# A planned four-layer graph network on one core: pair sums by transfers and VectorE norms in the last batch, setup work with its own priorities

## The chip, the cores and the metric

The kernel runs on one core of one Trainium2 chip. The metric is the device time of one execution in microseconds (us). A core has five engines that run their own instruction streams and wait for each other by semaphores: TensorE (PE, matmuls), VectorE (DVE), ScalarE (ACT), GpSimd (POOL) and SyncE (SP, which only issues transfers). All data are float32.

## The reference

Sixteen graphs (a batch each) of 1024 nodes with 256 features share one adjacency matrix of 1024 x 1024. Three graph attention layers with 4, 1 and 1 heads are followed by one transformer block with 8 heads; each layer gets the normalized, rectified features and is added to its input. Cut to what matters:

```python
def gat(h, adj, W, a, heads, slope, act):
    q = (h @ W).reshape(B, N, heads, D)
    e = (q . a_src)[:, :, None, :] + (q . a_dst)[:, None, :, :]
    e = where(adj > 0, leaky_relu(e, slope), -inf)
    return act(einsum('bijh,bjhd->bihd', softmax(e, axis=2), q))

def block(x, adj):
    q, k, v = split(x @ w_qkv)               # 8 heads of 32
    s = where(adj > 0, q @ k.T / sqrt(32), -1e9)
    x = layernorm(x + softmax(s) @ v, ln1_g, ln1_b)
    f = relu(x @ w1 + b1) @ w2 + b2
    return layernorm(x + f, ln2_g, ln2_b)

for layer in (gat0, gat1, gat2, block):      # elu, relu, elu, -
    x = x + layer(max(layernorm(x), 0))
```

## The kernel before

One function, `direct`, records the work of all sixteen batches, operation by operation, with the engine, an estimated duration, what is written and what is read (`pe`, `act`, `dve`, `pool` and `dma`, all by `Record.add`). `Record.schedule` (L193) then makes one order out of it: a list scheduling in which each engine takes, of the work that its model calls ready, the piece with the smallest key. The instructions are emitted in that order, so all queues stand as the planner left them. A key (`priority`, L140) is the batch number plus a value read off a line of knots by the position in the stream, minus a `LEAD` for the engine. The streams are `gat0`, `gat1`, `gat2` (the graph layers), `beside` (the first layer of batch 1, put beside batch 0), `steps` and `values` (the attention), `feed` (the second half of the block) and `last` (that half in the last batch). `PASS` is the delay that the model assumes between engines, `SLACK` an addition to a transfer's landing, `BIAS` the weight of a turn of PE between its tilings (whole array, or four columns of 32, called `col4`). The streams of the setup have fixed knots: weights of layer 0 and the adjacency (`setup`), weights of the others (`setup_later`), `signs`.

Two batches overlap: while one is in its graph layers, which multiply 128x128 weights by whole rows (L825 projections, L951 sums over neighbours in layers 1 and 2, L1038 and L1048 in layer 0), the other is in its attention. A graph layer hands to the next through `hn` (normalized rows, ACT, L533), PE transposes (L562), `hT` (their copies, ACT, L819), and the projection (L825), from which ACT makes the node terms `e` (L836) and `rt` (L897).

The attention of a batch has 32 steps: 2 head groups g of 4 heads, 2 halves hf of the query nodes, 8 blocks jt of 128 key nodes. A step makes four score products (L1417), their exponentials on ACT (L1441) into two tiles of 128x1024 from the ring `r_pa`, two multiplications by the mask on DVE (L1450), and one quad of 32-column products with the values (L1274). The denominators are quads of the same kind against a tile of ones. `run_of` (L1282) says how many steps one such quad serves: 8 in most batches, for which DVE adds tiles (L1301, L1309) and GpSimd issues accumulating transfers (L1318) into `sums`; 1 in the last batch, which adds nothing and issues a ones quad in each step.

After the attention `feed` normalizes (`turn`), makes the two products (L1517) and adds. `back` then turns each pair of row tiles back: transposes into a PSUM bank, copies with a row sum on ACT (L1609), squares on ACT (L479), the inverse root (L491 on DVE, L499 on POOL), and for each row tile a product with the gain (L1628) and one that adds the row of `xr` (L1641), which a transfer brought from DRAM (L1577) and L1583 adds a constant to. A last transfer stores it (L1650).

Behind the planned order stand a few instructions that make a flag from range checks: a matmul into the first shared PSUM bank (L1754), a sum and a comparison on DVE (L1756, L1757). All engines load the flag (L2309) and branch around a general version, which does not run here.

Of the kernel before, what the change touches and what calls it, by code (L numbers as in the profile page):

```python
# [16 lines left out]
AF = mybir.ActivationFunctionType  # L17
# [99 lines left out]
PASS = {"pe": 0.184, "act": 0.255, "dve": 0.2, "pool": 0.13, "dma": 0.0}  # L117
# [30 lines left out]
class Record:  # L148
# [165 lines left out]
SLACK = 0.962  # L314
KNOTS = {
# [3 lines left out]
    "beside": (-5.886, -0.218, 3.926, -4.339, 3.82),  # L319
    "values": (-2.1, -3.167, -2.515, -3.878, -1.376, 0.819, 4.772, 4.031, -0.727),  # L320
    "steps": (-0.731, 1.092, 1.111, 1.525, 1.942, 1.949, 3.509, 2.697, 0.422),
    "feed": (2.466, 7.301, 1.215, 1.509, 2.436, 1.431, -2.979, 1.844, 1.385),
    "last": (5.718, 3.017, 3.751, 2.762, 4.403, 4.069, 2.002, 6.755, 6.465),
}
BIAS = 3.565
LEAD = {"act": 3.258, "dve": -0.77}
# [33 lines left out]
def direct(ctx, tc, flag, x, adj, gat_w, gat_a, w_qkv, ln1_g, ln1_b, ln2_g, ln2_b, w1, b1, w2, b2, out):  # L360
# [328 lines left out]
    def signs():  # L689

        rec.stream(0, (0.9, 1.6), False)
        for it in range(NT):
            again = r_yT.new()
            a_i = again.t.rearrange("p a n -> p (a n)").bitcast(I32)
            dma(
                1.8,
                1.7,
                lambda: nc.sync.dma_start(a_i, adj[it * P : (it + 1) * P, :]),
                [again],
                [],  # L700
            )
# [436 lines left out]
    def attention(b, xt, b_mv, b_rstd):  # L1138
# [131 lines left out]
        pas, accs, sums = {}, {}, {}  # L1270
# [11 lines left out]
        def run_of(g, hf):  # L1282

            return 1 if b == NB - 1 else NT
# [4 lines left out]
        for n in range(len(steps) + LAG):  # L1289
            m = n - LAG  # L1290
            if m >= 0:
# [4 lines left out]
                if jt % run == 1:  # L1296
# [106 lines left out]
            if n < len(steps):  # L1403
# [5 lines left out]
                pts = [r_pa.new() for _ in range(2)]  # L1409
# [50 lines left out]
        watch(b_rec, b_rec.t, 1)  # L1460
        return hn

    def feed(b, x3, hn):
# [105 lines left out]
        def back(hf):  # L1569
            yT = yTs[hf]  # L1570
            for it in (hf * TH, hf * TH + 2):
# [34 lines left out]
                for k in range(2):  # L1606
                    act(
                        act_us(C) + 100e-3,
                        lambda: nc.scalar.activation(  # L1609
                            z_t[:, k, :], pz()[:, k, :], AF.Copy, accum_out=mvz.t[:, k, 0:1]  # L1610
                        ),
                        [z(k), mvz(k)],
                        [g],
                    )
                refs = [mvz(0), mvz(1)]
                spread_of(
                    [z_t[:, k, :] for k in range(2)],
                    [z(k) for k in range(2)],
                    mvz.t[:, :, 0],
                    mvz.t[:, :, 1],  # L1620
                    refs,
                )
                inverse_of_squares(mvz.t[:, :, 0], mvz.t[:, :, 1], rstdz.t, refs, rstdz, False)
                for k in range(2):
# [12 lines left out]
                        [mvz(k)],  # L1637
# [26 lines left out]
    def begin(b):  # L1664
# [3 lines left out]
        for hf in range(2):  # L1668
# [7 lines left out]
                b - 1.0,  # L1676
# [47 lines left out]
    graph(0, states[0], 0, first=True)  # L1724
# [626 lines left out]
```

## Time and profile before

| what | us |
|---|---|
| three runs | 3969.0, 3971.94, 3972.6 |
| median | 3971.94 |
| the profiled execution | 3968.2 |
| its span in the profile | 3966.4 |
| PE, from its first matmul to its last | 12.59 to 3955.56 |
| a period of the middle (two overlapping batches) | 241 |

The span runs from the first to the last event of the profile, and 1.8 us of the execution's time lie outside it. The mean granted clock of PE is 0.997 of full speed. Times in the views count from the start of the span. PEld is the weight load of PE, which runs beside its matmuls. The end of a matmul is modelled in the profile, so a wait can hide in a record that looks long. The groups that the change touches, in the list by costliest group and in the list of transfers (columns: line, engine, operation, tiles and shapes, count, then busy us, mean ns, then idle ahead of it and what ended it; for transfers the size of one and the us to its landing):

```profile
L1441 ACT ACTIVATE pa<-sc 128x512 f32<-128x512 f32 x2048 | 1099.7, 602 | 375.4 <-PE sc L1417 263.7
L1450 DVE TENSOR_TENSOR pa<-pa,mask 128x1024 f32<-128x1024 f32 x1024 | 1225.3, 1215 | 84.2 <-ACT pa L1441 83.0
L1318 POOL DMA_DIRECT2D sums<-pa x360 | 317.4, 882 | 1124.1 <-DVE pa L1450 324.5
L1274 PE MATMUL bank<-pa,va 128*32 128x512 f32 x4096 | 533.4, 599 | 1.0 <-DVE pa L1450 1.0
...
sums<-pa POOLq DMA_DIRECT2D x360, 512.0 KB, 5.0
```

### The profile page before, as it was taken

The numbers are of one execution on the slowest core, as the hardware profiler recorded it, in microseconds if no ns is written. First come the engines' busy times: TensorE is split into PE (matmuls) and PEld (weight loads), VectorE is DVE, ScalarE is ACT, GpSimd is POOL, SyncE is SP. The second block draws the span as 40 slices with busy tenths as digits, with TensorE's granted clock in tenths as the row PEclk, the third lists the DMA queues.
The fourth block names the chain that finished last, engine by engine and source line by source line (L and its number), as shares of the span: only waits on it lengthen the run. The fifth ranks groups of instructions, "written<-read, shape, count | busy, mean of one in ns | idle before, by whom it ended". The sixth has DMA issues, their size and how long they took to land. (4 is left out here: it accounts for less than half of the span.)

```text
span 3966.4 us, 64316 instructions
## 1 busy us (share of the span) xinstructions
PE 3915.6 (99%) x22946; PEld 2325.5 (59%) x22946; DVE 3616.0 (91%) x6134; ACT 2659.1 (67%) x6643; POOL 819.1 (21%) x751
## 2 busy tenths in 40 slices
PE   8999999999999999999999999999999999999998
PEld 4566566564665646566565665646656465665644
DVE  7769998999989999999999989999899999999976
ACT  5367577675766757577675776757667575775676
POOL 1002122221212212122121222212122131221210
PEclk9999999999999999999999999999999999999999
DMA  3156575555745556465465755557455564654652
GB/s 132 46 144 140 129 168 120 134 128 129 172 115 135 131 126 157 118 164 124 118 146 131 165 120 133 130 129 171 117 131 132 129 157 118 158 123 111 148 133 69
DMA packets 245946, 523.55 MB, mean 132 GB/s; under 512 B 26736, under 2 KB 61808, under 8 KB 245616
## 3 DMA queue, kind: packets, MB, share of 16 engines
q1 hardware_dynamic: 193776, 330.58, 29.5%
q0 software_dynamic: 51840, 188.77, 24.7%
q8 instruction: 183, 3.00, 0.3%
q14 instruction: 147, 1.20, 0.1%
HBM read 229.45 MB, written 101.06 MB: 83 GB/s over the span
## 5 line engine op out<-in xcount | busy, mean ns | idle before, releaser
L1441 ACT ACTIVATE pa<-sc 128x512 f32<-128x512 f32 x2048 | 1099.7, 602 | 375.4 <-PE sc L1417 263.7
L1450 DVE TENSOR_TENSOR pa<-pa,mask 128x1024 f32<-128x1024 f32 x1024 | 1225.3, 1215 | 84.2 <-ACT pa L1441 83.0
L924 DVE SCALAR_TENSOR_TENSOR pt<-row,e,mask 128x512 f32<-128x512 f32 x1472 | 1011.5, 742 | 43.4 <-DMA row<-rd 33.0
L951 PE MATMUL bank<-qb,pt 128*128 128x257 f32 x4096 | 952.2, 381 | 3.8 <-ACT rt L897 3.2
L951 PEld LDWEIGHTS bank<-qb,pt 128*128 128x128 f32 x4096 | 770.1, 189 | 168.6 <-ACT pa L1441 12.6
L1417 PE MATMUL sc<-qs,ks 128*128 128x512 f32 x2048 | 743.6, 467 | 3.1 <-ACT pa L1441 2.8
L1318 POOL DMA_DIRECT2D sums<-pa x360 | 317.4, 882 | 1124.1 <-DVE pa L1450 324.5
L1274 PE MATMUL bank<-pa,va 128*32 128x512 f32 x4096 | 533.4, 599 | 1.0 <-DVE pa L1450 1.0
L1417 PEld LDWEIGHTS sc<-qs,ks 128*128 128x128 f32 x2048 | 368.6, 189 | 189.2 <-issue 73.0
L1038 PE MATMUL bank<-pt,qb 128*32 128x512 f32 x3840 | 462.4, 597 | 3.4 <-DVE rec L1094 2.9
L1309 DVE TENSOR_TENSOR sums<-sums,pa 128x1024 f32<-128x1024 f32 x360 | 433.9, 1215 | 9.8 <-DMA sums<-pa 9.2
L825 PE MATMUL bank<-w_aug,hT 128*128 128x259 f32 (+1 forms) x1504 | 376.2, 394 | 5.1 <-DVE w_aug L641 2.7
L825 PEld LDWEIGHTS bank<-w_aug,hT 128*128 128x128 f32 x1504 | 277.5, 191 | 124.3 <-ACT hT L819 19.1
L499 POOL TENSOR_TENSOR rstd<-rstd,neg_half 128x4 f32<-128x4 f32 x94 | 152.0, 1617 | 794.6 <-DVE rec L971 472.6
L1038 PEld LDWEIGHTS bank<-pt,qb 128*32 128x32 f32 x3840 | 114.7, 110 | 269.0 <-issue 204.3
L1274 PEld LDWEIGHTS bank<-pa,va 128*32 128x32 f32 x4096 | 110.5, 109 | 254.1 <-issue 215.9
L979 ACT ACTIVATE ex<-bank,rec 128x256 f32<-128x256 f32 x256 | 121.0, 478 | 203.8 <-DVE rec L971 203.0
L1048 PE MATMUL bank<-pt,e 128*32 128x512 f32 x1920 | 252.2, 592 | 0.0
L1188 PE MATMUL sc<-hTa,wqkv_sb 128*128 128x512 f32 x512 | 243.8, 599 | 0.7 <-ACT hTa L1173 0.3
L533 ACT ACTIVATE hn<-xh,mv,rstd 128x256 f32<-128x256 f32 x376 | 199.8, 597 | 12.2 <-DVE mv L523 10.5
L479 ACT ACTIVATE waste<-xh,mv 128x256 f32<-128x256 f32 x376 | 191.6, 510 | 8.2
L514 POOL TENSOR_TENSOR rstd<-rstd,neg_half 128x4 f32<-128x4 f32 x66 | 86.7, 1313 | 496.1 <-DVE rstd L511 488.2
(153 smaller groups left out, 4565.5 us busy)
## 6 DMA issues: line engine op xcount, KB each, us to landing
sums<-pa POOLq DMA_DIRECT2D x360, 512.0 KB, 5.0
ks<-hl SPq DMA_DIRECT2D x256, 256.0 KB, 4.4
qs<-hl SPq DMA_DIRECT2D x256, 256.0 KB, 4.8
row<-rd SPq DMA_DIRECT2D x184, 256.0 KB, 3.3
hl<-hi SPq DMA_DIRECT2D x128, 256.0 KB, 3.3
hl<-lo SPq DMA_DIRECT2D x128, 256.0 KB, 3.6
xh<-in_x_dram SPq DMA_DIRECT2D x32, 512.0 KB, 3.9
x<-xh SPq DMA_DIRECT2D x32, 512.0 KB, 2.7
```

The source lines that it names most:

```text
L825: nc.tensor.matmul(g.t[:, : C + 3 * H], hT.t[:, ct, k * P : (k + 1) * P], w_aug[l][:, ct, :], start=ct == 0, stop=ct == CT - 1,)
L924: lambda: nc.vector.scalar_tensor_tensor(pt.t, row.t, e3[:, 2, jt // TH, h, jt % TH : jt % TH + 1], mask[:, jt, hf * HALF : (hf + 1) * HAL ...
L951: nc.tensor.matmul(g.t[:, : D + 1], pts[jt].t[:, k * P : (k + 1) * P], qb[:, jt, 0, :], start=jt == 0, stop=jt == NT - 1,)
L1038: nc.tensor.matmul(g.t[u * D + d : u * D + d + D3, :], qb[:, j, h + u, d : d + D3], pts[u][j - jt].t, start=j == 0, stop=j == NT - 1,)
L1048: nc.tensor.matmul(gd.t[c : c + D3, :], one(jt + k, h + u).to_broadcast([P, D3]), pts[u][k].t, start=jt == 0, stop=jt == NT - 2,)
L1188: nc.tensor.matmul(sc.t, wqkv_sb[:, ct, c0 : c0 + P], hT.t[:, ct, hf * HALF : (hf + 1) * HALF], start=ct == 0, stop=ct == CT - 1,)
L1274: nc.tensor.matmul(ac.t[r * D3 : (r + 1) * D3, :], columns(r), of_head(r), start=first, stop=last,)
L1309: lambda: nc.vector.tensor_add(ss.t, ss.t, pt.t),
L1318: lambda: nc.gpsimd.dma_start(ss.t, pt.t, accum_op=ALU.add),
L1417: nc.tensor.matmul(scs[r - r0].t, ks.t[:, r, jt * P : (jt + 1) * P].bitcast(F32R), q.t[:, r, :].bitcast(F32R), start=True, stop=True,)
L1441: lambda: nc.scalar.activation(pt.t[:, v, :], sc.t, AF.Exp, scale=1.0 / math.sqrt(D3)),
L1450: lambda: nc.vector.tensor_mul(pt.t, pt.t, mask[:, jt : jt + 1, i0 : i0 + HALF].to_broadcast([P, 2, HALF]),),
```

## The change

There are four parts. The planner's constants and nearly all knots have other values, and the setup's streams have knots of their own: `prepare` (weights of layer 0), `flags` (the adjacency), `later`, `signs`, and `first` for the first layer of batch 0. The transfers that bring x for batch 0 have the key -9.0 and not -1.0. In the last batch `run_of` is 2 for the first head group: the tiles of an odd step are added to those of the even step by two accumulating transfers that GpSimd issues, 512 KB each, and one ones quad serves both; the even steps' tiles come from six tiles lent by rings that are no longer used by then. In the second head group a ones quad still serves one step. For the last two row tiles of the last batch (`whole`) DVE takes mean and variance from PSUM with bn_stats and bn_aggr, and the product with the gain reads PSUM and subtracts the mean; the two ACT copies and the two squares of that pair are gone.

```diff
--- before.py
+++ after.py
@@ -114,7 +114,7 @@
 
 
 WEIGHT = {"pe": 1.0, "dve": 0.3}
-PASS = {"pe": 0.184, "act": 0.255, "dve": 0.2, "pool": 0.13, "dma": 0.0}
+PASS = {"pe": 0.187, "act": 0.284, "dve": 0.216, "pool": 0.13, "dma": 0.0}
 
 
 class Port(float):
@@ -311,19 +311,24 @@
 
 
 BEHIND, HELD = 2.0, 1.35
-SLACK = 0.962
+SLACK = 0.878
 KNOTS = {
-    "gat0": (-10.592, -9.852, -9.404, -9.422, -4.685, -5.744, -2.501, -5.476, -8.387),
-    "gat1": (-1.314, -0.409, 0.269, 0.767, 0.801, 0.716, 1.107, 1.18, 1.068),
-    "gat2": (0.968, -0.933, -0.332, -0.095, 0.667, 0.376, 1.511, 2.244, 1.831),
-    "beside": (-5.886, -0.218, 3.926, -4.339, 3.82),
-    "values": (-2.1, -3.167, -2.515, -3.878, -1.376, 0.819, 4.772, 4.031, -0.727),
-    "steps": (-0.731, 1.092, 1.111, 1.525, 1.942, 1.949, 3.509, 2.697, 0.422),
-    "feed": (2.466, 7.301, 1.215, 1.509, 2.436, 1.431, -2.979, 1.844, 1.385),
-    "last": (5.718, 3.017, 3.751, 2.762, 4.403, 4.069, 2.002, 6.755, 6.465),
+    "prepare": (-8.171, -25.204, -1.219),
+    "flags": (-1.972, 28.969, 31.434),
+    "later": (-3.058, -13.974, -19.276),
+    "signs": (9.615, 1.252, 2.905),
+    "first": (-33.677, -26.463, -11.613, -10.505, -4.473, -51.659, -18.668, -16.537, -6.288),
+    "gat0": (-11.671, -11.56, -7.573, -11.755, -6.35, -7.559, -3.8, -7.279, -7.121),
+    "gat1": (-1.318, -0.26, 0.293, 0.732, 0.82, 0.753, 1.148, 1.366, 1.233),
+    "gat2": (0.538, -0.372, 0.011, -0.014, 0.518, 0.041, 1.546, 1.925, 1.743),
+    "beside": (-5.462, -0.695, 4.93, -2.997, 3.186),
+    "values": (-2.004, -2.881, -2.02, -3.934, -1.847, 0.835, 4.775, 3.429, -0.703),
+    "steps": (-0.94, 1.05, 1.057, 1.547, 1.962, 2.299, 2.791, 2.536, 1.391),
+    "feed": (2.215, 6.339, 2.027, 1.413, 2.389, 1.61, -3.1, 1.598, 2.903),
+    "last": (7.027, 1.257, 3.242, 4.245, 5.763, 6.015, 2.958, 7.404, 7.821),
 }
-BIAS = 3.565
-LEAD = {"act": 3.258, "dve": -0.77}
+BIAS = 3.466
+LEAD = {"act": 3.86, "dve": -1.129}
 
 SWITCH = {
     ("full", "col4"): 0.137,
@@ -688,7 +693,7 @@
 
     def signs():
 
-        rec.stream(0, (0.9, 1.6), False)
+        rec.stream(0, KNOTS["signs"], False)
         for it in range(NT):
             again = r_yT.new()
             a_i = again.t.rearrange("p a n -> p (a n)").bitcast(I32)
@@ -711,15 +716,15 @@
 
 
     def setup():
-        rec.stream(-3.0, (0.0, 1.0), False)
+        rec.stream(0, KNOTS["prepare"], False)
         prepare(0)
-        rec.stream(-0.9, (0.0, 0.1), False)
+        rec.stream(0, KNOTS["flags"], False)
         nat = r_ks.new()
         for it in range(NT):
             neighbours(it, nat)
 
     def setup_later():
-        rec.stream(-0.5, (0.0, 0.3), False)
+        rec.stream(0, KNOTS["later"], False)
         prepare(1)
         prepare(2)
         dma(
@@ -1267,7 +1272,14 @@
         b_rec = r_reca.new()
         rc = b_rec.t.rearrange("p (a b t h) -> p a b t h", a=CT, b=2, t=TH)
         steps = [(g, hf, jt) for g in range(CT) for hf in range(2) for jt in range(NT)]
-        pas, accs, sums = {}, {}, {}
+        pas, accs, sums, outs = {}, {}, {}, {}
+        r_even = r_pa
+        if b == NB - 1:
+            owners = [r_qb.new(), r_hT.new(), r_hn.new()] + [r_sums.new() for _ in range(2)]
+            t_qb, t_hT, t_hn, *more = (o.t for o in owners)
+            tiles = [t_qb[:, k * N : (k + 1) * N].rearrange("p (a n) -> p a n", a=2) for k in range(2)]
+            tiles += [t_hT, t_hn.rearrange("p t c -> p (t c)").rearrange("p (a n) -> p a n", a=2)] + more
+            r_even = Lent(tiles, owners)
 
         def quad(ac, of_head, columns, first, last):
             for r in range(HG):
@@ -1281,7 +1293,7 @@
 
         def run_of(g, hf):
 
-            return 1 if b == NB - 1 else NT
+            return (1 if g == 1 else 2) if b == NB - 1 else NT
 
         rec.stream(b, KNOTS["steps"])
         GROUP = 2
@@ -1293,7 +1305,19 @@
                 if jt == 0:
                     accs[g, hf] = [r_bank.new(), r_bank.new()]
                 run = run_of(g, hf)
-                if jt % run == 1:
+                if run == 2 and jt % 2:
+                    sums[g, hf] = pas[m - 1]
+                    for ss, pt in zip(pas[m - 1], pas[m]):
+                        dma(
+                            2.4,
+                            2.0,
+                            lambda: nc.gpsimd.dma_start(ss.t, pt.t, accum_op=ALU.add),
+                            [ss],
+                            [pt],
+                            us=1.135,
+                            engine="pool",
+                        )
+                elif jt % run == 1:
                     sums[g, hf] = [r_sums.new() for _ in range(2)]
                     for ss, p0, p1 in zip(sums[g, hf], pas[m - 1], pas[m]):
                         dve(
@@ -1406,7 +1430,7 @@
                     f(*at)
                 pas[n] = []
                 i0 = hf * HALF
-                pts = [r_pa.new() for _ in range(2)]
+                pts = [(r_pa if jt % 2 else r_even).new() for _ in range(2)]
                 pas[n] = pts
                 for r0 in range(0, HG, GROUP):
                     scs = [r_sc.new() for _ in range(GROUP)]
@@ -1458,6 +1482,8 @@
                                 mask_of(hf),
                             )
         watch(b_rec, b_rec.t, 1)
+        if b == NB - 1:
+            r_even.give_back()
         return hn
 
     def feed(b, x3, hn):
@@ -1603,38 +1629,47 @@
 
                 q = it % TH // 2 if PARTS == 2 else 0
                 pe(0.109 * 2 * CT, turn_back, [g], [yT((co, q)) for co in range(CT)])
-                for k in range(2):
-                    act(
...
-                inverse_of_squares(mvz.t[:, :, 0], mvz.t[:, :, 1], rstdz.t, refs, rstdz, False)
+                whole = PARTS == 2 and it == TH + 2
+                if whole:
+                    refs = [mvz(0), mvz(1)]
+                    for k in range(2):
+                        st = r_st["f"].new()
+                        dve(0.315, lambda: nc.vector.bn_stats(st.t, pz()[:, k, :]), [st], [g])
+                        dve(0.08, lambda: nc.vector.bn_aggr(mvz.t[:, k, :], st.t), [mvz(k)], [st])
+                    inverse(mvz.t[:, :, 0], mvz.t[:, :, 1], rstdz.t, refs, rstdz, False)
+                else:
+                    for k in range(2):
+                        act(
...
+                    inverse_of_squares(mvz.t[:, :, 0], mvz.t[:, :, 1], rstdz.t, refs, rstdz, False)
                 for k in range(2):
                     u, xs = z_t[:, k, :], xr.t[:, k, :]
                     dve(
                         stt_us(C),
                         lambda: nc.vector.scalar_tensor_tensor(
                             u,
-                            u,
+                            pz()[:, k, :] if whole else u,
                             mvz.t[:, k, 0:1],
                             rows["g2"][:, 0, :],
-                            op0=ALU.add,
+                            op0=ALU.subtract if whole else ALU.add,
                             op1=ALU.mult,
                         ),
                         [z(k)],
-                        [mvz(k)],
+                        [mvz(k)] + ([g] if whole else []),
                     )
                     dve(
                         stt_us(C),
@@ -1673,7 +1708,7 @@
                 lambda: nc.sync.dma_start(xt.half(hf), x_b[:, s, :]),
                 [xt(it) for it in range(hf * TH, (hf + 1) * TH)],
                 AFTER_ROWS[1 if b == 1 else 3] * (b in (1, 2)),
-                b - 1.0,
+                b - 1.0 if b else -9.0,
             )
         for hf in range(2):
             its = range(hf * TH, (hf + 1) * TH)
@@ -1721,7 +1756,7 @@
 
     setup()
     states = [begin(0)]
-    graph(0, states[0], 0, first=True)
+    graph(0, states[0], 0, knots=KNOTS["first"], first=True)
     setup_later()
     states.append(begin(1))
     borrowed = lent()
```

More of the change, by code (lines that the diff above doesn't have):

```diff
@@ L1605, in back @@
                 pe(0.109 * 2 * CT, turn_back, [g], [yT((co, q)) for co in range(CT)])
-                for k in range(2):
-                    act(
[L1608 to L1613, printed above, removed]
-                    )
[L1615 to L1622, printed above, removed]
-                inverse_of_squares(mvz.t[:, :, 0], mvz.t[:, :, 1], rstdz.t, refs, rstdz, False)
+                whole = PARTS == 2 and it == TH + 2
[9 more added lines that the diff above has]
+                        act(
+                            act_us(C) + 100e-3,
+                            lambda: nc.scalar.activation(
+                                z_t[:, k, :], pz()[:, k, :], AF.Copy, accum_out=mvz.t[:, k, 0:1]
+                            ),
+                            [z(k), mvz(k)],
+                            [g],
+                        )
+                    refs = [mvz(0), mvz(1)]
+                    spread_of(
+                        [z_t[:, k, :] for k in range(2)],
+                        [z(k) for k in range(2)],
+                        mvz.t[:, :, 0],
+                        mvz.t[:, :, 1],
+                        refs,
+                    )
+                    inverse_of_squares(mvz.t[:, :, 0], mvz.t[:, :, 1], rstdz.t, refs, rstdz, False)
                 for k in range(2):
```

## The prediction

> **What bounds the kernel now.** I read the busy times first, then the busy time by windows, then the waits of PE, then timelines of the places that the change touches. The busy times:
>
> ```profile
> PE 3915.6 (99%) x22946; PEld 2325.5 (59%) x22946; DVE 3616.0 (91%) x6134; ACT 2659.1 (67%) x6643; POOL 819.1 (21%) x751
> ```
>
> PE sets the time. Work taken from DVE, ACT or POOL is worth something only where PE waits for it. Where that is shows in the windows (columns: stretch, its length, then busy us and instructions of PE, PEld, DVE, ACT, POOL; then clock and DMA):
>
> ```profile
> 0.00:12.50 12.50, 0.00 (x0) 0.00 (x0) 7.81 (x38) 2.11 (x3) 1.78 (x8) 1.00 0.81 284
> 12.50:120.00 107.50, 97.89 (x743) 48.39 (x744) 88.88 (x184) 56.23 (x157) 10.60 (x12) 0.98 0.29 94
> 120.00:225.00 105.00, 101.16 (x577) 68.15 (x578) 76.61 (x168) 44.14 (x117) 5.73 (x10) 0.95 0.17 56
> 225.00:300.00 75.00, 71.01 (x306) 43.76 (x308) 48.52 (x70) 49.98 (x118) 8.08 (x11) 0.98 0.66 166
> ...
> 1140.00:1381.00 241.00, 240.72 (x1415) 143.81 (x1415) 226.12 (x381) 165.56 (x417) 54.83 (x48) 1.00 0.57 136
> ...
> 3750.00:3956.00 206.00, 200.06 (x1136) 103.51 (x1134) 154.02 (x250) 142.96 (x328) 21.32 (x21) 1.00 0.38 96
> 3956.00:3966.40 10.40, 0.00 (x0) 0.00 (x0) 4.69 (x12) 2.58 (x11) 2.16 (x2) 0.56 0.27 86
> ```
>
> A middle period of 241 us (13 alike) has PE idle for 0.28 us. The ends have idle: 12.5 ahead of the first matmul, 9.6 up to 120, 3.8 up to 225, 4.0 up to 300, 5.9 in the last 206, and 10.4 behind the last matmul. The waits of PE name the single causes (sum, times, longest):
>
> ```profile
> PE bank L562 <- DVE rstd L511: 12.6, 1, 12.6
> PE bank L951 <- ACT rt L897: 3.2, 13, 0.2
> PE bank L1038 <- DVE rec L1094: 2.9, 1, 2.9
> ...
> PE bank L825 <- DVE w_aug L641: 2.7, 1, 2.7
> PE bank L562 <- ACT hn L533: 1.8, 1, 1.8
> ```
>
> The sum is made against the profiled execution: 3968.2 us, of which the span is 3966.4; the median of the runs is 3971.94, 3.7 above it, and I add that at the end.
>
> **Start.** The key of the first loads moves x ahead of W and a on SP: two issues, at 0.76 and 1.26, so x is issued and lands 1.0 us sooner, and W and a as much later. DVE now does the row statistics ahead of the weight preparation, which stood ahead of them from 4.98 to 7.67. In the built order two groups of adjacency transposes on PE, not four, and two mask copies on ACT, not three, stand ahead of the first hT. The first exponentials of the node terms are now at:
>
> ```profile
> 20.44 2.02 ACT L681 CAST mask<-bank 128x512 uint8<-128x512 f32 x4
> 22.33 0.21 ACT L836 ACTIVATE e<-bank 128x12 f32<-128x12 f32 x1
> ```
>
> With the same durations in the new order: statistics start at 6.7 instead of 7.67; from the first to hn's shift (7.67 to 11.48) it was 3.81, less one statistic of 0.4, so hn starts at 10.2 instead of 11.67; its four take 2.07; eight transposes 1.04 and two copies 1.07 end at 14.4; the second hn group takes 2.07 and four mask copies 2.02, with 0.2 between, so the first e stands at 18.7: 3.6 us sooner. The first weighted adjacency (DVE L924, at 31.20) follows by the same step at 27.6. From there to 93 DVE is the slower engine (88.88 busy of 107.5), so the lead is carried. The preparation of layer 1's weights, for which PE waits 2.7 us at 119.86, now has 6.1 us less DVE work ahead of it by the sum of the two orders' durations (87.5 against 93.6), PE has 5.0 less ahead of its projection (84.6 against 89.6). I take −4.7 at that point: −3.6 from the head and 1.1 of the wait. Bounds: −1.0 (the x issue alone) and −6.1 (all of DVE's lead).
>
> Then batch 1's first-layer sums stand between batch 0's layers 1 and 2 in the new order, where PE waits 0.60 for e at 193.76 and 1.84 for hn at 195.87: −2.5 for both, bounds 0 and −4.0 (a further 1.5 of the slow L825 behind them). The stretch 225–300, where PE waits on exponentials, keeps nearly its order: 0, bounds ±4.0, its idle.
>
> **Middle.** All knots change, but the built PE order has 13 periods with the same work, 95% of it in the same places, DVE 87%, ACT 82%. The weak place is the handover from layer 1 to 2, where ACT makes hT between two groups of hn:
>
> ```profile
> 1323.53 1.29 PE L1417 MATMUL sc<-qs,ks 128*128 128x512 f32 x4
> 1324.75 2.06 PE L1274 MATMUL bank<-pa,va 128*32 128x512 f32 x8
> 1326.73 4.12 PE L825 MATMUL bank<-w_aug,hT 128*128 128x259 f32 x16
> ...
> 1324.17 0.56 ACT L819 COPY hT<-bank 128x512 f32<-128x512 f32 x1
> 1324.63 2.08 ACT L533 ACTIVATE hn<-xh,mv,rstd 128x256 f32<-128x256 f32 x4
> 1326.61 0.56 ACT L819 COPY hT<-bank 128x512 f32<-128x512 f32 x1
> ```
>
> The quad pair of 8 at 1324.75 shows 2.06, and elsewhere 1.07 (at 1317.97): 0.99 is a hidden wait for the copy at 1326.61. The new order places that copy behind the same hn group, and one exponential more (0.60) ahead of the first copy, while it takes the first half's transposes earlier. I take 0. Bounds: 13 × −0.99 = −12.9, and 13 × 0.60 = +7.8.
>
> **Fewer denominators.** For the first head group of the last batch a ones quad (4 columns × 2 records) is issued every second step: 8 quads fewer of 16. A chain of waits gives the price: "PE bank L1274" x16 takes 1.85, x24 2.71, so 0.86 for 8: 8 × 0.86 = −6.9. They ran in a stretch where PE is 97% busy, so this counts in full. Two more visits to the 32-column mode in the order cost 0.32 each (two scores, a quad pair and the turns, 1318.99 to 1320.63, is 1.64, less 2 × 0.23 for the scores and 0.86): +0.6. The pairs are now added by 16 transfers on POOL's queue, 0.88 each to issue (317.4 us for 360). Behind them on POOL stand only the pow instructions (three between 3923 and 3940), and POOL is 10% busy there: 21.32 of 206. The six tiles lent are idle by then. From the last score of an odd step to its ones quad the built order puts 9.6 to 16.9 us of PE work, median 13.7. Needed are one exponential 0.60, one multiply 1.21, two issues 1.76 and the landing:
>
> ```profile
> DMA to landing us min/median/max: 4.5/5.1/9.6
> ```
>
> So 8.7, and the shortest has 0.9 to spare before any queueing on DVE: +0.5, bounds 0 and +14.4 (third rival).
>
> The issues of 24 such adds in the middle period take 859 to 917 ns while DVE is 94% busy: nothing holds them there, and only the landing's tail to 9.6 leaves room for a hold. The Trainium skill (page "SBUF — State Buffer", section "SBUF: two separate sides") speaks against the change here: a transfer issued from GpSimd waits for its descriptors while VectorE holds the port that both share. By that rule one multiply of 1.21 more would stand ahead of each of 8 pairs and cost at most 9.7, and the sum would be −2.3 in place of −12.0; by the issue rows it costs nothing.
>
> **Tail.** For the last two row tiles DVE takes mean and variance straight from PSUM: 2 bn_stats and 2 bn_aggr more (about 1.0 by 0.40 and 0.17 each at 8.42), and ACT loses two copies (0.38 and 0.19 for the accumulator's read) and two squares (0.51 and 0.19). But the last chain hangs on the xr transfer:
>
> ```profile
> 3953.14 3.66 DMA xr<-x
> 3956.82 0.69 DVE xr L1583
> ```
>
> so DVE has the same eight products and two adds left after 3956.8, and ends within ±0.7 of 3961.6. Second, those transposes use and hold the bank that the flag's matmul (L1754) also writes, so the flag now comes after DVE's last products, not at 3955.78. The engines' branches of 3.4 to 3.7 us, which ran beside the tail, start later: +1.0, bounds −0.5 and +2.5.
>
> **Sum.** −4.7 −2.5 +0 −6.9 +0.6 +0.5 +1.0 = −12.0: 3956.2 profiled, 3960 for the median.
>
> **Rivals.**
> 1. The start's lead is lost: PE reaches the score stretch at 225–300 earlier but waits longer there for the same exponentials. For: 4.0 idle there. Against: those exponentials also start earlier. Left: −6.9 +0.6 +0.5 +1.0 = −4.8: 3967.
> 2. Slower: the handover of layers 1 to 2. If the second hT copy comes one more hn group later (2.08), PE has two scores (0.46) to fill: 1.6 × 13 = +21: 3981. It decides from 1.55 us in each period. For: ACT's order differs most (82%). Against: I see only one more exponential.
> 3. The paired sums land late: with the longest landing, 9.6, and 2 us of queueing on DVE 15.2 is needed, and the eight distances (14.4, 16.1, 12.9, 12.5, 16.9, 13.5, 13.9, 9.6) fall short by 0.8, 0, 2.3, 2.7, 0, 1.7, 1.3 and 5.6, together 14.4: 3974.
> 4. More comes back: the reordering also takes the idle of 225–300 (4.0) and of the last 206 us (5.9), the rt waits (3.2) and the rec wait (2.9): −16.0 more, 3944.
>
> **How the numbers follow.** Forecast 0.50, rivals 0.15, 0.12, 0.07, 0.16. A measurement of this kernel can tell about 0.2%, 7.9 us: faster is below 3964.0, slower above 3979.9. The forecast's own range is 3952 to 3966 (the start's and tail's bounds together), so of its 0.50 0.42 is faster, 0.08 the same; rival 1 gives 0.13 same, 0.02 faster; 2 gives 0.10 slower, 0.02 same; 3 0.05 same, 0.02 slower; 4 0.16 faster. Faster 0.60, same 0.28, slower 0.12. The range 3943 to 3976 leaves out rival 2 and some of 4, under 0.2.
>
> **What would show it.** Start: first e near 18.7, PE's wait on w_aug under 1.6. Quads: PE's 32-column instructions down by 64 records, 6 to 7 us less PE work in the last 250 us; a wait of PE on sums landing would show rival 3. Middle: 241.0 per period; 242.5 would show rival 2. Tail: 10 to 13 us from PE's last transposes to the end. The prediction is wrong if the middle's periods differ by over 0.5 us, which I can't read from an order.

## The result, and the profile after

The changed kernel takes 3982.14 us (median of 14 runs, 3977.32 to 3985.63) against 3971.53 of the kernel before (14 runs, 3966.99 to 3973.85): ratio 1.0026, 95% interval 1.0018 to 1.0035. It is slower by some 10 us, and lies outside the predicted range of 3943 to 3976. Its profiled execution took 3979.5, with a span of 3977.7.

The busy times of the changed kernel, from the head of its page, and its busy time by windows, with the same columns as before:

```profile
PE 3917.1 (98%) x22882; PEld 2326.3 (58%) x22882; DVE 3615.6 (91%) x6138; ACT 2666.6 (67%) x6634; POOL 769.9 (19%) x767
```

```profile
225.00:300.00 75.00, 69.37 (x311) 41.73 (x310) 53.61 (x69) 46.67 (x111) 8.21 (x12) 0.95 0.76 182
...
1140.00:1381.00 241.00, 240.18 (x1409) 141.85 (x1408) 224.02 (x379) 164.66 (x410) 45.58 (x48) 1.00 0.59 134
1381.00:1622.00 241.00, 240.52 (x1416) 143.95 (x1415) 226.28 (x381) 166.37 (x417) 52.08 (x48) 1.00 0.58 136
```

PE has its 64 records less (22,882 for 22,946), as forecast, but it is no longer only PE's work that fills the span. The window 1140 to 1381 holds fewer instructions of PE (1409 for 1415): that period takes longer than 241 us, the next does not. The list of VectorE's waits shows what is new (first line of each; sum, times, longest), before and after:

```profile
DVE sums L1309 <- DMA sums<-pa: 9.2, 5, 4.4
```

```profile
DVE sums L1333 <- DMA sums<-pa: 35.2, 33, 2.6
...
```

L1333 is L1309 of before, the addition of an odd step's tile to a sum into which an accumulating transfer has just been made. Its waits for the landing rose from 5 to 33. The transfers themselves did not become slower: the view of the tile gives minimum, median and maximum of all landings, before and after,

```profile
DMA to landing us min/median/max: 4.4/5.0/11.1
```

```profile
DMA to landing us min/median/max: 4.4/4.9/10.9
```

To see where the time goes, I compared the times at which PE starts the same piece of work in both traces (the 1st record of every 128 of the products of layers 1 and 2 with the neighbours' weights; changed minus before, us):

```text
at (before)    530.1   850.5  1332.6  2055.6  2537.4  3020.4  3741.3   last transposes   end of span
changed         -2.7    -0.2    +1.3    +1.6    +4.8    +7.7    +8.8        +9.7            +11.3
```

So the start brings 3 us, the middle loses 12 in irregular steps, the last batch loses 1, though it has 6.9 us less of PE's work, and the tail loses 1.6.

### The profile page after: what moved, and what is told of

Read it like the earlier page. It is cut to its first block, busy times and chain, and to the rows that moved or that the text cites. A ratio compares the mean times of both kernels' runs of the same rounds, so it can differ in the third digit from the quotient of the medians.

```text
span 3977.7 us, 64227 instructions
## 1 busy us (share of the span) xinstructions
PE 3917.1 (98%) x22882; PEld 2326.3 (58%) x22882; DVE 3615.6 (91%) x6138; ACT 2666.6 (67%) x6634; POOL 769.9 (19%) x767
## 4 chain that ended last, share of the span: by engine, by line
PE 79%; DVE 11%; DMA 3%; ACT 3%; issue 3%; POOL 1%; SPq 0%; DVEq 0%; ACTq 0%; POOLq 0%
PE bank L956 17%; PE bank L1286 12%; PE sc L1441 10%; PE bank L1043 9%; PE bank L830 8%; PE bank L567 6%; PE bank L1053 4%; PE sc L1193 4%; PE bank L1543 4%; DVE pt L929 3%; DVE pa L1474 3%; PE sc L1231 2%; DMA sums<-pa 2%; POOL rstd L504 1%; PE sc L567 1%
## 5 line engine op out<-in xcount | busy, mean ns | idle before, releaser
L1465 ACT ACTIVATE pa<-sc 128x512 f32<-128x512 f32 x1984 | 1056.2, 600 | 348.7 <-PE sc L1441 217.5
L1474 DVE TENSOR_TENSOR pa<-pa,mask 128x1024 f32<-128x1024 f32 x992 | 1189.9, 1217 | 54.2 <-ACT pa L1465 50.2
L1286 PE MATMUL bank<-pa,va 128*32 128x512 f32 x3968 | 516.7, 599 | 0.6 <-DVE pa L1474 0.5
L1333 DVE TENSOR_TENSOR sums<-sums,pa 128x1024 f32<-128x1024 f32 x360 | 434.8, 1218 | 35.6 <-DMA sums<-pa 35.2
L830 PE MATMUL bank<-w_aug,hT 128*128 128x259 f32 (+1 forms) x1504 | 366.7, 390 | 12.3 <-ACT hT L824 6.1
L830 PEld LDWEIGHTS bank<-w_aug,hT 128*128 128x128 f32 x1504 | 279.5, 190 | 115.6 <-ACT hT L824 19.8
L504 POOL TENSOR_TENSOR rstd<-rstd,neg_half 128x4 f32<-128x4 f32 x94 | 166.1, 1767 | 706.0 <-DVE rstd L496 407.7
L1202 ACT CAST hi<-sc 128x512 fp32r<-128x512 f32 x128 | 75.7, 591 | 151.3 <-PE sc L1193 137.6
```

What stands on the lines that cost most here:

```text
L830: nc.tensor.matmul(g.t[:, : C + 3 * H], hT.t[:, ct, k * P : (k + 1) * P], w_aug[l][:, ct, :], start=ct == 0, stop=ct == CT - 1,)
L1286: nc.tensor.matmul(ac.t[r * D3 : (r + 1) * D3, :], columns(r), of_head(r), start=first, stop=last,)
L1333: lambda: nc.vector.tensor_add(ss.t, ss.t, pt.t),
L1465: lambda: nc.scalar.activation(pt.t[:, v, :], sc.t, AF.Exp, scale=1.0 / math.sqrt(D3)),
L1474: lambda: nc.vector.tensor_mul(pt.t, pt.t, mask[:, jt : jt + 1, i0 : i0 + HALF].to_broadcast([P, 2, HALF]),),
```

## The experiments

Most runs put the same pieces of work in a written-out order. Setting one of the planner's constants back gives another plan everywhere, not the changed one less one part. But both plans have finished exactly the same pieces at two places: after 1,688 pieces (about 420 us) and after 15,928 (about 3600 us). There an order can be cut and continued with the other kernel's. The edit is the same in each such run, and only the list differs:

```diff
     with tc.manual_schedule():
-        for w in rec.schedule():
+        for w in rec.replay(ORDER):
             w.emit()
```

`replay` takes each piece in the order of the list, and gives it its tile as `schedule` does. All results below are ratios to the kernel before, with 95% intervals, and the difference that the ratio makes of 3971 us.

**The parts, one by one.** Start in the changed order, the rest as before:

> The kernel before, with its first 1,688 pieces of work (up to some 420 us) in the order of the changed kernel and all later ones in its own. If the start is worth what stands between the two traces at that point (3.3 us earlier at the 513th record of the first layer's sums, 425.2 against 421.9), 3.3 us less than before. If the predicted 7.2 was right and the changed middle ate the rest, 7 less. If the lead is lost as soon as the old middle follows, no difference.

0.9990 (0.9981 to 0.9999): 4.0 us less. Only the middle in the changed order:

> The kernel before, with only the pieces from 420 to 3600 us (14,240 of them) in the order of the changed kernel. If the middle's order costs what the traces show between these places (from 3.3 us ahead to 8.8 behind), 12 us more than before, in some periods and not in others, with some 35 waits of VectorE's adds (the second addition to sums) for the landing of their transfers, against 5 to 8. If the new order's loss came only from the state in which the changed start left the queues, no difference. If the handover of layer 1 to 2 is what costs, over 1 us in every period, without a wait for landings.

1.0026 (1.0016 to 1.0037): 10.3 us more, as much as the whole change loses, with 28 waits for landings of 31.1 us. Only the end changed, with its pair sums, its rows and its order:

> The changed kernel's last batch (pair sums by transfers, rows normed by VectorE, its order from 3600 us on) behind start and middle in the order of before. If the eight ones quads taken away (6.3 us with the turns) only made PE wait for ScalarE's exponentials, as the changed trace's stalls of 9 us more behind 3750 say, and the tail costs 1.6: 1 to 3 us more than before. If the quads' time is gained and was lost elsewhere: 4 to 6 us less than before.

0.9998 (0.9989 to 1.0007): no difference. Start and end changed and the old middle between them:

> The changed kernel, start and end in its own order, with the middle (420 to 3600 us) in the order of before. If the three parts add up as measured one by one (-4.2, 0, -0.4): 4 to 5 us less than before. If the end's gain needs the changed middle in front of it, or the start's lead is lost behind it: within 2 of before.

0.9989 (0.9980 to 0.9998): 4.4 less. The parts add up, and the middle is the loss. This version is faster than both kernels, by no more than its start.

**The middle: which addition.** A first try moved every addition that the plan had put close behind its transfer:

```diff
 order of the middle, 78 additions at L1333
-  issue of the transfer, ..., addition, next VectorE instruction
+  issue of the transfer, ..., next VectorE instruction, addition
```

> As the run with only the middle in the new order, but each of the 78 second additions that the planner set less than 7.3 us behind the issue of the transfer that they need stands one or two VectorE instructions later (1.2 on the mean). If the loss is these additions' waits for landings: at most 4 us more than before in place of 12, and the waits for landings down to about 10. If it is anything else in the new order: 10 to 14 us more than before, like the run without the moves.

1.0057 (1.0044 to 1.0071): 22.6 us more, a miss. The plan's distances are not the chip's: the waits stayed (24, 37.2 us), and PE waited for mask products that were now late. One addition, the ninth of each period (see below), still had only 7.3 us of room in this run and alone waited 19.8 us in twelve periods. So I read the distances from the traces, addition by addition. Each period has 24. One, the ninth, stands out: VectorE's turn for it came 13.0 us after the issue of its transfer before, and 7.5 in the changed order, and the transfer lands after 5.7 to 9.7 there. Five or six other transfers are issued within 3 us of it in every period, among them loads of key halves and of xr (256 KB each). The second, twelfth and twenty-first transfers of a period, with no other transfer that near, land after 4.4 to 5.1. No run takes the loads away, so that they are what holds the ninth up is likely, and not shown. One late landing of the changed kernel, in its timeline of POOL, VectorE and PE:

```profile
785.30 0.86 POOL L1342 DMA_DIRECT2D sums<-pa  x1 [6.02 <-DVE rec L976]
...
792.06 0.74 DVE L1588 SCALAR_TENSOR_TENSOR yT<-bank,col_b,yT 128x512 f32<-128x512 f32 x1
795.10 1.22 DVE L1333 TENSOR_TENSOR sums<-sums,pa 128x1024 f32<-128x1024 f32 x1 [2.29 <-DMA sums<-pa]
796.24 0.74 DVE L1588 SCALAR_TENSOR_TENSOR yT<-bank,col_b,yT 128x512 f32<-128x512 f32 x1
...
796.00 0.27 PE L567 MATMUL bank<-ident,yT 128*128 128x128 f32 x1
797.04 0.98 PE L567 MATMUL bank<-ident,yT 128*128 128x128 f32 x7 [0.77 <-DVE yT L1588]
```

The transfer issued at 785.30 lands after 9.7 us. VectorE stands still for 2.29 us before the addition at 795.10, the product for yT behind it is late, and PE waits for yT at 797.04. Three tests of this one addition:

```diff
 order of the changed middle, 13 periods
-  ninth addition, five VectorE instructions (3.7 us)
+  five VectorE instructions (3.7 us), ninth addition
```

> The kernel before with the middle in the changed kernel's order, except that in each of 13 periods one VectorE instruction stands five places later: the ninth of the period's 24 second additions to sums, which had 7.5 us between the issue of its transfer and VectorE's turn, and 13.0 in the old order, while the transfer lands after 5.6 to 10.1 us. If this one addition's wait (10.3 us of VectorE in twelve periods) is what makes the middle slower, 1 to 5 us more than before in place of 11 (the two others, of 4 to 9 us in all, stay). If the wait is hidden and the rest of the new order costs, 9 to 13 more. If any addition that moves later costs, as in the run with 78 moves, above 13 more.

1.0021 (1.0011 to 1.0030): 8.3 more. The waits of the ninth addition were gone, but each period was now 0.4 to 0.7 us longer: the move has a price of its own, about what it saves. This run could not decide. The reverse move in the kernel before:

```diff
 order of the kernel before, 13 periods
-  nine VectorE instructions (5.8 us), ninth addition
+  ninth addition, nine VectorE instructions (5.8 us)
```

> The kernel before, with nothing changed but that ninth addition, nine VectorE places earlier in each of 13 periods, so that it has some 7.3 us of room and not 13.0. If the wait for the landing is the cause, it waits up to 3 us in half of the periods, about 10 us in all, and the kernel is 5 to 11 us slower than before. If the new middle's loss has another cause, within 2 us of before.

1.0045 (1.0032 to 1.0059): 17.9 us more, above the 5 to 11 expected, by one instruction in each period. In its trace the periods in which the transfer landed in time are as long as before, within 0.1 us, so here the move by itself costs nothing. Where it landed late PE lost as much as VectorE waited, or more (4.2 and 4.8 us for waits of 2.8 and 3.4); why more stays open. And without any move, a transfer of half the size:

```diff
-  nc.gpsimd.dma_start(ss.t, pt.t, accum_op=ALU.add)
+  nc.gpsimd.dma_start(ss.t[:, :1], pt.t[:, :1], accum_op=ALU.add)
```

> As the run with only the middle in the new order, which was 11 us slower than before, with no instruction moved, but the ninth of each batch's 24 accumulating transfers takes half of its tile (256 KB; one head's denominators lack one block of keys for half of the rows). It then lands 1 to 2 us sooner and meets its addition more often. If the addition's wait for this landing makes the middle slow, 2 to 6 us more than before; if that wait is a mark of something else, 9 to 13 more.

1.0007 (0.9998 to 1.0016): 2.8 more in place of 10.3, with the order of each engine as it was. VectorE's two largest waits for transfers, with only the middle changed and then in this run (L1401 is the addition in both):

```profile
DVE pt L1016 <- DMA row<-rd: 34.6, 15, 5.3
DVE sums L1401 <- DMA sums<-pa: 31.1, 28, 3.3
```

```profile
DVE pt L1016 <- DMA row<-rd: 38.3, 19, 5.2
...
DVE sums L1401 <- DMA sums<-pa: 27.0, 30, 3.0
```

The smaller transfer could also have helped by leaving the queues freer for all others. The wait for `row` did not shrink, which speaks against that. The waits of the additions fell by only 4.1 in all, but those of the ninth fell by 5.5 (below); the others, mostly of the fourteenth and the sixteenth addition, cost little. With these two treated likewise:

> As the run with only the middle in the new order and one of its transfers halved (2.8 us more than before), with the other two that VectorE waits for in each period halved as well (the fourteenth and the sixteenth of 24; two blocks of keys are missing for one more head). If landings are all that is wrong with the new middle, within 2 us of before. If a part of its loss has another cause, the 3 us stay.

1.0004 (0.9995 to 1.0013): 1.6 more, not told from nothing, and not from the 2.8 either: whether a small part of the loss has another cause stays open. Executions differ here: the ninth addition waited 7.4 us in this one, with the same half transfer. The other traces tell the ninth addition's part, period by period: the wait of the ninth addition, summed over twelve periods, and how much later than in the kernel before PE came to the same work across these places (both us):

```text
                           waits   PE later
changed kernel              10.9     10.5
middle alone                10.4     10.6
ninth addition earlier      11.4     15.6
half transfer                4.9      2.8
```

In the changed kernel the single periods have waits of 2.3, 0.1, 1.4, 0, 0.1, 0.6, 2.1, 1.5, 0.2, 2.6, 0, 0, and delays of 1.9, 0.6, 1.1, 0, 0.1, 0.1, 1.9, 1.1, 0.9, 2.2, 0.8, -0.2.

**The end: where the quads went.** With eight quads put back beside the eight that are left:

```diff
-  lambda: quad(accs[g, hf][1], ..., jt == run - 1, jt == NT - 1)
+  lambda: [quad(accs[g, hf][1], ..., first, last) for again in range(1 + (run == 2))]
```

> As the run with the changed end behind the old start and middle, but each ones quad of the first head group in the last batch is issued twice, so that PE has eight quads more, as many as before the change; the sums of these four heads in the last batch come out doubled. If PE waits there for ScalarE's exponentials anyway, the eight cost 0 to 3 us over the run without them. If PE sets the pace, they cost 6 to 7.

1.0026 (1.0017 to 1.0036): 10.3 more than before, and 11 over the run without them. That spoke for PE as the bound. But taken out of the order of before,

```diff
-  lambda: quad(accs[g, hf][1], ...)
+  lambda: None if run == 1 and g == 0 and jt % 2 else quad(accs[g, hf][1], ...)
```

> The kernel before in its own order, with the eight ones quads of the odd steps of the last batch's first head group left out, so that these denominators lack half of their terms; no transfer takes their place. If PE sets the pace in that stretch, 6 to 8 us less than before. If ScalarE's exponentials do, 0 to 3 less.

0.9995 (0.9986 to 1.0004): 2 us less, not told from nothing. The trace says more. Every engine's order is that of before up to the first quad left out, and yet PE was 5.8 us behind the trace of before at 3500 to 3590 us. Some 3.6 of that arose near 280 us, where the granted clock was 0.74 between 275 and 295, against 0.91. At its last score product PE was only 1.0 behind. So in the order of before some 4.8 of the 6.9 us came in the last batch, which the interval (5.6 less to 1.6 more) allows. The new knots' order for the end, with all quads:

> The kernel before, with all its ones quads and ScalarE's rows, but from 3600 us on in the order that the planner makes of it with the changed constants and knots. In the run with the whole changed end, eight quads fewer brought 0.4 us and not 6.9, though eight quads put back there cost 9. If the new knots are what takes the rest, this is 4 to 7 us slower than before. If the pair sums themselves do (their landings, or the longer way from exponentials to sums), within 2 us of before.

1.0002 (0.9993 to 1.0011): no difference, so this order costs nothing by itself. The pair sums alone, planned with the old knots:

> The kernel before with nothing but the pair sums by transfers (every second ones quad of the first head group left out in the last batch, sixteen transfers, six lent tiles), planned with the old constants and knots. If the pair sums cost more than they bring unless the knots are made for them, 0 to 6 us slower than before. If they are worth their quads, 4 to 7 us faster.

1.0034 (1.0021 to 1.0048): 13.5 more. The waits of PE between 3740 and 3980 us in this run (sum, times, longest):

```profile
PE sc L1436 <- DMA ks<-hl: 5.1, 1, 5.1
PE bank L1281 <- DMA qb<-pa: 4.8, 3, 2.2
```

Here the transfers do collide: the loads of keys (ks) that took 4.0 to 5.9 us to land in this stretch before took up to 11.6, and PE waited for it, and for the landings of pair sums. Between 3880 and 3900, in and behind these waits, the granted clock was 0.68, and 1.00 before; that is a part of the 13.5 too. With the new knots, is crowding also what takes the gain? The whole end, without the transfers:

```diff
-  lambda: nc.gpsimd.dma_start(ss.t, pt.t, accum_op=ALU.add)
+  lambda: None
```

> As the run with the changed end behind the old start and middle (0.4 us less than before), with the sixteen pair transfers of the last batch left out and nothing moved: eight ones quads fewer, and half of the terms missing in these denominators. If the transfers' crowding of the DMA queues (share 0.92 to 1.07 between 3820 and 3900 us, 0.32 to 0.56 before) takes back what the quads bring, 5 to 9 us less than before. If ScalarE's exponentials limit that stretch with or without transfers, 0 to 3 less, like the run that only left the eight quads out.

1.0000 (0.9991 to 1.0009): no gain either. The DMA share between 3860 and 3880 fell from 1.04 to 0.47, and the order of each engine stayed. So with the new knots crowding is not it. The timeline of this run shows a part of what is, PE first, then ACT:

```profile
3841.72 1.03 PE L1379 MATMUL bank<-hn,ones 128*32 128x512 f32 x4
3844.11 1.96 PE L1534 MATMUL sc<-qs,ks 128*128 128x512 f32 x4 [1.36 <-ACT hT L1558]
3846.00 1.06 PE L1379 MATMUL bank<-sums,ones 128*32 128x512 f32 x8
...
3842.51 0.57 ACT L1474 COPY ota<-bank 128x512 f32<-128x512 f32 x1
3842.97 0.51 ACT L577 ACTIVATE waste<-fz,mvz 128x256 f32<-128x256 f32 x1
3843.38 0.19 ACT L577 ACTIVATION_READ_ACCUMULATOR waste<-fz,mvz 128x1 f32 x1
3843.47 1.07 ACT L1558 ACTIVATE hT<-sc 128x512 f32<-128x512 f32 x2
3844.43 1.09 ACT L1558 ACTIVATE hn<-sc 128x512 f32<-128x512 f32 x2
```

ACT is busy without a gap with the rows of batch 14, then with exponentials; PE's next four scores wait from some 3842.2 to 3844.11 for a score bank that an exponential must free. In the run with the new order and all quads PE passes the same place with a ones quad in each step:

```profile
3842.38 1.20 PE L1509 MATMUL sc<-qs,ks 128*128 128x512 f32 x4
3843.51 1.06 PE L1366 MATMUL bank<-pa,va 128*32 128x512 f32 x8
3844.39 1.04 PE L1366 MATMUL bank<-pa,ones 128*32 128x512 f32 x8
3845.36 0.73 PE L1509 MATMUL sc<-qs,ks 128*128 128x512 f32 x2
```

Counting in these two traces, from 3740 us on, the distance between the starts of PE's instructions above their undisturbed price, it is 12.0 us with all quads and 19.0 without eight of them: 7.0 more, for 6.9 of work less. The waits of PE name 2.4 of them as waits for score banks that an exponential frees, between 3800 and 3900 us without the quads; with all quads there are none:

```profile
PE sc L1534 <- ACT hT L1558: 1.7, 2, 1.4
PE sc L1534 <- ACT pa L1558: 0.7, 1, 0.7
```

Another part is the clock. Without the quads PE was granted half of full speed for 3.4 us from 3802.5, so that it lost up to 1.7 us; with all quads the clock was 1.00 from 3740 to 3940. Four products for the block's second half (128x512) took 3.13 us there, and 1.98 with all quads. The window of both, first without the eight quads (last three columns: clock, DMA share, GB/s):

```profile
3800.00:3820.00 20.00, 19.40 (x72) 12.71 (x73) 7.46 (x18) 15.76 (x30) 1.02 (x1) 0.91 0.70 178
```

```profile
3800.00:3820.00 20.00, 19.68 (x87) 11.86 (x90) 8.37 (x16) 14.89 (x28) 1.02 (x1) 1.00 0.70 181
```

The changed kernel has two such stretches in its last batch, from 3806.0 and from 3877.6. The rest of the 7.0 stands in records that look long, and no view names its cause. So the quads were in part PE's work while ACT caught up; for the whole 7.0 that is not shown. Eight quads put back in pairs, at the places of the other eight, are not the same, so that run does not price the eight that were taken out.

**Tail and sum.** The rows alone:

> The kernel before with nothing but the last two row tiles normed by VectorE. If the flag's place decides, its matmul shares the bank of the last transposes as in the changed kernel, the flag comes behind VectorE's last products, and from the last transposes to the end it takes 14.2 us in the profile (12.6 before, 12.4 with the same rows and another bank): 1 to 2 us slower than before. If the rows bring more than the flag costs, 12 us or less there and up to 1 faster.

1.0004 (0.9995 to 1.0013): not told from nothing by the times. In its profile the stretch from the last transposes to the end is 14.6 us, against 12.6 before, 14.2 in the changed kernel, and 12.4 in the run with the changed end behind the old middle, where another bank fell to the last transposes and the flag stood at 3956.1. One trace does not settle so little: with the end of before unchanged, the run with only the start changed took 14.0 there, as VectorE waited 2.20 us for xr in place of 0.90, and the run with only the middle changed 12.3. Last, the start of the change with the new order for the end but without pair sums and rows:

> The kernel before in its own code, with the changed start's order up to 420 us, its own order to 3600 us, and behind it the order of the changed knots (its ones quads and ScalarE rows kept). If the parts add up, 4 to 6 us less than before, level with the run that had start and end of the change.

0.9992 (0.9983 to 1.0001): 3.2 us less, level with the start alone.

## Why the prediction was wrong

**The step that failed: "Middle. ... I take 0."** It measured +12 in the trace of the changed kernel and +10.3 alone. I looked at the handover from layer 1 to 2, counted that no work was added, and read the likeness of the orders (PE 95%, VectorE 87%) as likeness of the time. The price lay in a place that I did not look at in the middle: the distance between the issue of a transfer and the instruction that needs it. I had that very sum, issue to use against landing, for the sixteen new transfers of the last batch (third rival), and did not apply it to the 360 old ones, whose additions the new slack and knots moved as well. The landing's median of 5.1 hid that the ninth lands after 6.6 to 10.0 in the kernel before too; there it had 13.0 us of room.

**The second rival** named the handover, 1.6 us in each of 13 periods. That its total, 3981, stands beside the measured 3982 is luck: it had the sign, but twice the size for the middle (21 us for 10 to 12), on top of gains of 12 that came only in part. Nor had it the mechanism: PE's wait for hT there is 0.4 us in each of 13 periods, where it had been 0.2 for rt, and the quiet periods are no longer than before. It was also priced in every period, where the real loss comes only where a landing is late.

**Fewer denominators: -6.9 +0.6.** The claim that "this counts in full" because PE is 97% busy was wrong. In the order of before the eight quads less brought 4.8 us in the trace and 2 by the times; with the new knots' order they brought nothing, and PE stood 7.0 us longer between its instructions. Of these 2.4 are named as waits for exponentials, up to 1.7 are the clock, and the cause of the rest stays open. A share of 97% over 206 us says nothing of a reserve: ACT runs without a gap in parts of the stretch. My +0.5 for late landings is near: with the new knots PE waits 0.3 us for a pair's landing (qb, between 3800 and 3900), though these transfers land after 4.8 to 11.6 us, not 5.1.

**Start: -7.2.** It gave 3.3 in the trace at 425 us, and 4.0 alone (0.4 to 7.5 by the interval, which does not rule out 7.2; the rows do). The first e is not at 18.7:

```profile
11.13 2.08 ACT L538 ACTIVATE hn<-xh,mv,rstd 128x256 f32<-128x256 f32 x4 [4.82 <-DVE mv L528]
13.82 0.58 ACT L686 CAST mask<-bank 128x512 uint8<-128x512 f32 x1 [0.62 <-PE bank L567]
14.68 0.58 ACT L686 CAST mask<-bank 128x512 uint8<-128x512 f32 x1 [0.27 <-PE bank L567]
...
20.74 0.22 ACT L841 ACTIVATE e<-bank 128x12 f32<-128x12 f32 x1
```

hn starts at 11.13 and not at 10.2, and the mask copies wait for transposes that I let run beside it; the head gains 1.6, not 3.6. The wait for layer 1's weights did not shrink to under 1.6 but grew to 4.9 (PE came sooner, the weights not as much), and in the window 225 to 300 PE idles 5.6 us, where it was 4.0: part of the first rival, that the lead is spent there on exponentials, came true. Between 120 and 225, where I took -2.5, PE's idle did fall, from 3.84 to 1.17.

**Tail: +1.0.** In the trace it is +1.6, and both sides of the mechanism named are there: VectorE's chain from the transposes to its last product is 1.1 us shorter (6.7 against 7.8), and the flag behind it costs more. The end of the changed kernel's timeline:

```profile
3968.57 1.67 DVE L1676 SCALAR_TENSOR_TENSOR xr<-fz,rstdz,xr 128x256 f32<-128x256 f32 x4
3968.71 0.19 PE L1789 MATMUL bank<-good,ones_col 128*1 128x4 f32 x2 [3.91 <-DVE fz L1663]
3969.47 1.18 SPq L1685 DMA_DIRECT2D out_dram<-xr  x2
3970.15 0.14 DVE L1791 TENSOR_REDUCE n_good<-bank 1x1 f32<-1x4 f32 x1
3970.33 0.14 DVE L1792 TENSOR_SCALAR flag<-n_good 1x1 int32<-1x1 f32 x1
```

From the flag to the end are 7.2 us; before, the flag came at 3955.9, 10.5 before the end. As the same old end took 12.3 to 14.0 in three traces, 1.6 is within what executions differ by.

**The Trainium skill's rule** (page "SBUF — State Buffer", section "SBUF: two separate sides") was not what cost: the issues of the new transfers in the last batch take 859 to 1222 ns, for 859 to 917 in the middle period of before, so at most 0.36 us of one issue can be a hold by VectorE. The section says it of VectorE's two-port performance modes, and that `tensor_tensor`, as the multiplication by the mask is, has none; my estimate of 9.7 left that condition out.

By the parts measured one by one, -4.0 +10.3 -0.8 is 5.5, plus some 1.8 (an estimate, 14.2 less 12.4) for the flag that lay in another bank in the end's own run: 7.3, of the 10.3 by the ratio of the whole. The rest is within the intervals of the parts (3 to 4 us each way).

## What to carry to other kernels

For each instruction that waits for a transfer, read from the trace the time from the transfer's issue to that instruction's turn and set it beside the landing's whole spread at that place, not beside the median over all; an order that is 90% the same can have spent the room of a few of them. A share of 97% on the bounding engine is no promise that its work can be removed at full price: look whether the next engine runs without gaps in that stretch, and at the granted clock there. Before a difference of a few microseconds between two traces is put down to an edit, compare them at the last place where both orders are still the same: here two executions stood 5.8 us apart there. To find which part of a replanned program costs, cut and join orders where both have done the same work; resetting one constant makes a third program.

## What the runs showed of the hardware

The landing of one and the same transfer of 512 KB, the ninth of a period, varied from 5.7 to 9.7 us over twelve periods of the changed kernel's execution, with five or six other transfers issued within 3 us of it; transfers of the same size with none so near landed after 4.4 to 5.1. Half of the ninth (256 KB) landed after 4.4 to 8.7, so most of the spread does not come from its own size. Sixteen more such transfers in the last batch made the DMA share 1.04, where it is 0.47 without them (3860 to 3880 us, the changed end behind the old middle); in the changed kernel they landed after 4.8 to 11.6 us.

The granted clock of PE stood at half of full speed for stretches of 3.4 us and more, at other places in other executions; in one, four products that take 1.98 us took 3.13. The runs do not show what sets this off.
